# Bilinear feature interaction on one core: output buffers as pools of their own, eight instead of ten x blocks on GpSimd's queue, and one store split in two

## The chip, the core and the metric

The kernel runs on one core of a Trainium2 chip. The core has five instruction streams that run beside each other and meet only at semaphores: TensorE (PE, with its weight loads PEld), VectorE (DVE), ScalarE (ACT), GpSimd (POOL) and SyncE (SP). Three of them also start DMA transfers: SP, ACT and POOL each have a queue (in the profile q1 carries what SP starts, q10 what ACT starts, q0 what POOL starts), and all transfers run on the same 16 DMA engines. The metric is the time of one execution on the device in microseconds (us); lower is better.

## The reference

The input is x of shape [4096, 32, 64] (4096 rows of a batch, 32 fields, 64 numbers per field) and one 64x64 matrix W for each of the 496 pairs of fields i < j. For each row and each pair the kernel computes a vector of 64 numbers and writes them all:

```python
idx_i, idx_j = np.triu_indices(F, k=1)
vi = inputs[:, idx_i, :]
vj = inputs[:, idx_j, :]
vidots = jnp.einsum('bpd,pde->bpe', vi, W)
return vidots * vj
```

All numbers are float32. The inputs are 33.5 MB of x and 8.1 MB of W; the output is 4096 x 496 x 64 numbers, 520 MB. The output outweighs the input by more than ten to one.

## The kernel before, in words

The batch is cut into 16 blocks of 256 rows. A block holds two tiles, one row per partition each, so that there are 32 tiles of 128 rows. For one tile, all pairs (i, j) with the same i are neighbours in the output, so one product with field i against the matrices of several j gives up to 16 pairs at a time (a "step", L314: two matmuls, one for each half of the 64 result columns, into one PSUM buffer of two banks). The step's result is multiplied by the x fields j and lands in an output buffer in SBUF. For most steps DVE does this straight from PSUM (L330). For the first step of the fields i in `aside` (1, 3, 5, ..., 13), ACT copies PSUM to the output buffer (L327) and POOL multiplies there (L328), seven times for each tile.

Steps are gathered into groups of pairs; when a group is complete, SP stores it with one DMA (L335). The first three tiles (`LEAD = 3`) are cut into six groups each and run interleaved, group by group, while the weights still arrive. All later tiles are cut into four groups each of 118 to 127 pairs (3.8 to 4.2 MB per store) and run one after the other. Only the very first group of tile 0 is stored in two parts (`ends`).

The output buffers are all parts of one SBUF tile `ob` (L74), and `out_home` (L82) says by a running number n which part a group gets: three buffers in turn at first, four from n = 10 (`FOURTH`) to the end of the lead, and three larger ones from tile 3 on. The same tile also holds, in the beginning, the last raw rows of W and the reordered rows `rp` that TensorE transposes into the weight tile `wT`. The framework keeps track of which region of a tile an instruction reads and writes, and puts waits between them.

x lives in `xb`, five slots of one x tile each (L71). Blocks 0 and 1 are loaded by SP at the start. From then on, `loads` gives the moment: at the fifth step of the last tile of one pair of blocks (2e - 2 and 2e - 1), the next pair (2e, 2e + 1) is loaded. So there are seven such moments, e = 1 to 7. A block in the list `fifteen` (L110) is loaded by POOL with `load_fifteen`: one DMA of 120 partitions (L165), a tiny one over 17 partitions that turns POOL's queue on by one engine (`turn_engines`, L157), and two of the last 8 partitions. The code takes it that 120 partitions go to 15 of the 16 DMA engines, 8 rows of 16 KB each, so that one engine is spared, always the same. Any other block is loaded whole by ACT (L141), three steps later in the program. `slots_of` says which two slots a block takes. Before the change, the pairs at e = 1, 2, 4, 6 have one block on each queue (ACT the first, POOL the second), and the pairs at e = 3, 5, 7 have both blocks on POOL.

TensorE also transposes x: four fields' pairs at a time (L213), copied by ACT to a transposed buffer (L215 to L217) in two buffers of `xtb` (and, during the lead, in two more in slot 0 of `xb`).

The order of the instructions on each engine is the order of the program; the places of the loads, of the transposes (`AHEAD`) and of the weight work (`due`) are written out by hand. SP's queue holds nothing but loads at the start and then the stores in order; each store waits for the last DVE and POOL instruction of its part.

Of the kernel before, what the change touches and what calls it, by code (L numbers as in the profile page):

```python
# [8 lines left out]
F32 = mybir.dt.float32  # L9
# [3 lines left out]
def kernel(  # L13
# [17 lines left out]
    nc = tc.nc  # L31

    B, F, D = x.shape
    P = 128
# [5 lines left out]
    E2 = D // 2  # L40
    BANK = 512
    CH = BANK // E2
    RUN = 8
    p0 = [i * (F - 1) - i * (i - 1) // 2 for i in range(F)]
# [5 lines left out]
    wrows = list(zip(cuts[:-1], cuts[1:]))  # L50


    LEAD = 3
# [3 lines left out]
    for t in range(NT):  # L57
        b = lead if t < LEAD else later
        groups[t] = list(zip(b[:-1], b[1:]))
    cap0 = max(b - a for a, b in groups[0])  # L60
    cap1 = max(b - a for a, b in groups[LEAD])

    const = ctx.enter_context(tc.tile_pool(name="const", bufs=1))
# [5 lines left out]
    wT = const.tile([P, NP, E2], F32, tag="wT", name="wT")  # L69
    FD = F * D  # L70
    xb = const.tile([P, 5, FD], F32, tag="xb", name="xb")  # L71
    XT = 2 * (RUN // 2) * P
    xtb = const.tile([P, 2 * XT], F32, tag="xtb", name="xtb")
    ob = const.tile([P, 3 * cap1, D], F32, tag="ob", name="ob")  # L74

    FOURTH = 3 * len(groups[0]) - 8  # L80

    def out_home(n: int, later_: bool):  # L82
        if later_:
            o, c = (2 - n % 3) * cap1, cap1
        elif n < FOURTH:
            o, c = (0, 2, 1)[n % 3] * cap0, cap0
        else:
            k = 3 - (n - FOURTH) % 4
            o, c = k * cap0 if k < 3 else 3 * cap1 - cap0, cap0
        return ob[:, o : o + c, :]  # L90

    RAW, RP = P * E2 // D, 2 * BANK // D
    assert 3 * cap0 + RAW + 2 * RP <= 3 * cap1 and LEAD == 3 and FOURTH % 3 == 1

    xt_used = [0]

    def xt_home(t: int):
        n = xt_used[0]  # L100
        xt_used[0] += 1
        n = n % 4 if t < LEAD else n % 2
        mem, o = (xtb, n * XT) if n < 2 else (xb[:, 0], (n - 2) * XT)
        return mem[:, o : o + XT].rearrange("p (s u b) -> p s u b", s=2, b=P)

    fifteen = (3, 5, 6, 7, 9, 10, 11, 13, 14, 15)  # L110

    def slots_of(blk: int):
        e, second = divmod(blk, 2)
        if e == 0:
            return ((1, 2), (3, 4))[second]
        if e % 2 == 0:
            return ((2, 3), (1, 4))[second]
        if 2 * e in fifteen:
            return ((1, 3), (2, 0))[second]
        return ((1, 2), (3, 0))[second]  # L120

    def tile_of(t: int):

        blk, k = divmod(t, NB)
        a, b = slots_of(blk)
        return blk, k if a < b else 1 - k
# [5 lines left out]
    def x_tile(t: int):  # L132
        blk, k = tile_of(t)
        return x_block(blk)[:, k]
# [39 lines left out]
    wflat = w.rearrange("p d e -> p (d e)")  # L174
    EU = 2 * BANK // P
    NU = E2 // EU

    def raw_w(c: int):
        if c + 1 < len(wrows):
            a = wrows[c + 1][0]  # L180
            return wT[:, a : a + P, :].rearrange("p r e -> p (r e)")
        return ob[:, 3 * cap1 - RAW :, :].rearrange("p r e -> p (r e)")

    def load_w(c: int):
        a = wrows[c][0]
        nc.sync.dma_start(out=raw_w(c), in_=wflat[a : a + P])

    def order_w(c: int, k: int, copy):

        r = wrows[c][1] - wrows[c][0]  # L190
        o = cap0 + k * RP if c == 0 else 3 * cap1 - RAW - (1 + k % 2) * RP
        rp = ob[:, o : o + RP, :].rearrange("p r e -> p (r e)").rearrange("p (e h d) -> p e h d", h=2, d=D)
        src = raw_w(c)[:r].rearrange("p (d h e) -> p e h d", h=2, d=D)
        ins = copy(rp[:r], src[:, k * EU : (k + 1) * EU])  # L194
        if c > 0:
            tc.keep_in_program_order(ins)
        return rp
# [9 lines left out]
    def turn_x(t: int, q: int, copy):  # L207


        pt = psum.tile([P, RUN // 2, P], F32, tag="ps", name=f"ptx_{t}_{q}")  # L210
        for u in range(RUN // 2):
            f = q * RUN + 2 * u
            nc.tensor.transpose(pt[:, u, :], x_tile(t)[:, f : f + 2, :].rearrange("p f d -> p (f d)"), ident)  # L213
        xT = xt_home(t)
        copy(xT[:, 0], pt)  # L215
        copy(xT[D:, 1], pt[:D])  # L216
        copy(xT[:D, 1], pt[D:])  # L217
        return xT
# [58 lines left out]
    v, p, a = nc.vector.tensor_copy, nc.gpsimd.tensor_copy, nc.scalar.copy  # L277
    xT, rps = {}, {}
# [5 lines left out]
        if k == 3:  # L284
            xT[0, 0] = turn_x(0, 0, a)

    n_out = {}
    for s, (t, st) in enumerate(sched):
        blk, kt = tile_of(t)
        g, i, c0, m = steps[t][st]  # L290
        if s in loads:
            for b in (loads[s], loads[s] + 1):
                if b in fifteen:
                    load_fifteen(b)
        if s - 3 in loads and loads[s - 3] not in fifteen:
            tc.keep_in_program_order(load_x(loads[s - 3], nc.scalar))
        for what, *args in due.get(s, ()):
            if what == "x":
                xT[tuple(args)] = turn_x(*args, a)
            elif what == "turn":  # L300
                turn_w(*args, rps.pop(tuple(args)), a)
            else:
                c, k = args
                rps[c, k] = order_w(c, k, ((v, v, p, v), (v, v, p, a))[k % 2][c])

        base, end = groups[t][g]
        pa = p0[i] + c0
        if pa == base:
            ot = out_home(len(n_out), t >= LEAD)
            n_out[t, g] = ot  # L310
        ot = n_out[t, g]
        ps = psum.tile([P, 2, CH, E2], F32, tag="ps", name=f"ps_{s}")
        for h in range(2):
            nc.tensor.matmul(  # L314
                ps[:, h, :m, :],
                xT[t, i // RUN][h * D : (h + 1) * D, (i + h) % 2, i % RUN // 2, :],
                wT[h * D : (h + 1) * D, pa : pa + m, :],
                start=True,
                stop=True,
            )  # L320
        o = pa - base
        j = i + 1 + c0
        dst = ot[:, o : o + m, :].rearrange("p m (h e) -> p m h e", h=2)
        src = ps[:, :, :m, :].rearrange("p h m e -> p m h e")
        xj = x_tile(t)[:, j : j + m, :].rearrange("p m (h e) -> p m h e", h=2)
        if i in aside and c0 == 0:
            nc.scalar.copy(dst, src)  # L327
            nc.gpsimd.tensor_mul(dst, dst, xj)  # L328
        else:
            nc.vector.tensor_mul(dst, src, xj)  # L330

        ends = (p0[2], end) if (t, g) == (0, 0) else (end,)
        if pa + m in ends:
            n0 = p0[2] if len(ends) > 1 and pa + m == end else base
            nc.sync.dma_start(  # L335
                out=rows_of(out, blk).rearrange("(p k) n d -> p k n d", k=NB)[:, kt, n0 : pa + m, :],
                in_=ot[:, n0 - base : pa + m - base, :],
            )
# [28 lines left out]
```

## Time and profile before

| quantity | value |
|---|---|
| median of 5 runs | 1332.47 us (1330.3 to 1335.79) |
| profiled execution | 1330.3 us |
| its span, first to last instruction | 1328.5 us |
| bytes moved, mean rate | 563.17 MB, 424 GB/s |
| PE, DVE, ACT, POOL busy | 86%, 72%, 35%, 43% |
| mean granted TensorE clock | 0.948 |

The profile's page gives the busy share of each engine, then the span in 40 slices (the rows DMA and GB/s tell how busy the 16 DMA engines were in each slice and what they moved), the DMA queues, and the chain of work that ended last. Beside the page, the trace answers for any stretch of time: busy time of each engine, granted clock, mean busy share of the DMA engines and GB/s, and for each group of DMA issues the median time from issue to landing. A busy share of the DMA engines slightly over 1 in a stretch comes from packets that overlap a little. The trace also keeps each DMA packet with its start, length, size and queue. Each store ends with 16 packets of four bytes, one on each DMA engine, so their spread shows how far the 16 engines lie apart.

### The profile page before, as it was taken

Reading aid. Unit: us, or ns where it says so; the run is one execution under the profiler, and the core shown is the slowest. Engines: PE = TensorE matmul, PEld = TensorE weight load, DVE = VectorE, ACT = ScalarE, POOL = GpSimd, SP = SyncE. Lnnn points to the kernel's source line nnn. Section 1 sums busy time; section 2 is a strip of 40 time slices with the busy share of each in tenths; the row PEclk is TensorE's granted clock in tenths of the full one; section 3 lists DMA queues with packets and bytes.
Section 4 is the critical chain, followed back from the end, with each engine's and each line's share of the span. In section 5 each row is a group of like instructions: output and inputs, shape, how many; then the busy total and the mean of one; then the engine's idle time right before and its main releaser. Section 6 shows DMA issues by size and latency. Waiting matters only on the chain.

```text
span 1328.5 us, 17395 instructions
## 1 busy us (share of the span) xinstructions
PE 1141.2 (86%) x6644; PEld 600.3 (45%) x6644; DVE 951.3 (72%) x1287; ACT 471.3 (35%) x627; POOL 566.1 (43%) x276
## 2 busy tenths in 40 slices
PE   6999989997988978998788897798969988889884
PEld 4455445453444434444344444444434444444442
DVE  5679768774777766877577876678757777677773
ACT  4563324332333323333233332333323333233331
POOL 2861524445434444435344352444524445244440
PEclk9999989998999998999899999999989999889997
DMA  9999999999999999999999999999999999999998
GB/s 388 432 426 429 399 431 432 431 432 423 431 431 432 433 411 423 431 430 419 424 430 433 429 425 413 427 432 430 419 427 427 435 430 397 429 428 431 433 430 365
DMA packets 25170, 563.17 MB, mean 424 GB/s; under 512 B 3680, under 2 KB 3680, under 8 KB 4128
## 3 DMA queue, kind: packets, MB, share of 16 engines
q1 hardware_dynamic: 20448, 532.69, 93.9%
q0 software_dynamic: 4064, 21.00, 4.1%
q10 hardware_dynamic: 576, 8.39, 1.6%
q8 instruction: 52, 0.85, 0.2%
q14 instruction: 30, 0.25, 0.0%
HBM read 41.94 MB, written 520.09 MB: 423 GB/s over the span
## 4 chain that ended last, share of the span: by engine, by line
DMA 36%; PE 13%; DVE 5%; issue 3%; POOL 2%; ACT 2%; DVEq 0%; ACTq 0%; POOLq 0%
DMA out_dram<-ob 30%; PE ps L314 12%; DVE ob L330 5%; DMA xb<-in_r_inputs_dram 5%; POOL ob L328 2%; ACT ob L327 1%; PE ptx L213 1%; POOL xb L165 0%; POOL scratch L157 0%; ACT xtb L215 0%; ACT xtb L217 0%; ACT xtb L216 0%; DVEq L330 0%; ACTq L327 0%; DVEq L363 0%
## 5 line engine op out<-in xcount | busy, mean ns | idle before, releaser
L330 DVE TENSOR_TENSOR ob<-ps,xb 128x1024 f32<-128x1024 f32 (+4 forms) x1277 | 939.9, 791 | 345.5 <-DMA out_dram<-ob 176.0
L314 PE MATMUL ps<-wT,xtb 64*128 64x512 f32 (+15 forms) x5760 | 1013.1, 490 | 147.2 <-ACT ob L327 77.8
L328 POOL TENSOR_TENSOR ob<-ob,xb 128x1024 f32<-128x1024 f32 x224 | 528.5, 2364 | 734.4 <-ACT ob L327 717.9
L314 PEld LDWEIGHTS ps<-wT,xtb 64*128 64x128 f32 x5760 | 509.4, 195 | 613.5 <-DVE ob L330 230.3
L327 ACT COPY ob<-ps 128x1024 f32<-128x1024 f32 x224 | 226.8, 1012 | 479.7 <-PE ps L314 265.5
L215 ACT COPY xtb<-ptx 128x512 f32<-128x512 f32 x122 | 71.4, 585 | 315.5 <-PE ptx L213 315.5
L213 PE MATMUL ptx<-ident,xb 128*128 128x128 f32 x512 | 85.8, 291 | 8.6 <-DMA xb<-in_r_inputs_dram 6.6
L213 PEld LDWEIGHTS ptx<-ident,xb 128*128 128x128 f32 x512 | 55.2, 144 | 61.0 <-issue 31.7
L217 ACT COPY xtb<-ptx 64x512 f32<-64x512 f32 x122 | 71.0, 582 | 3.0
L216 ACT COPY xtb<-ptx 64x512 f32<-64x512 f32 x122 | 70.4, 577 | 3.0
L314 PE MATMUL ps<-wT,xb 64*128 64x512 f32 (+15 forms) x244 | 41.4, 460 | 1.0 <-ACT ob L327 0.3
L314 PEld LDWEIGHTS ps<-wT,xb 64*128 64x128 f32 x244 | 20.4, 186 | 17.4 <-issue 6.0
L204 PE MATMUL ptw<-ident,ob 128*128 128x128 f32 (+1 forms) x128 | 18.6, 298 | 10.9 <-DVE ob L194 10.4
L204 PEld LDWEIGHTS ptw<-ident,ob 128*128 128x128 f32 (+1 forms) x128 | 15.5, 157 | 16.7 <-issue 13.5
L165 POOL DMA_DIRECT2D xb<-in_r_inputs_dram x30 | 18.9, 631 | 0.0
L205 ACT COPY wT<-ptw 128x1024 f32<-128x1024 f32 (+1 forms) x15 | 14.9, 992 | 9.6 <-PE ptw L204 9.5
L194 DVE COPY ob<-wT 128x1024 f32<-128x1024 f32 (+1 forms) x7 | 7.1, 1040 | 8.9 <-DMA wT<-in_L_rec_W_dram 8.9
L157 POOL DMA_DIRECT2D scratch<-in_r_inputs_dram x12 | 11.1, 924 | 0.3 <-issue 0.3
L215 ACT COPY xb<-ptx 128x512 f32<-128x512 f32 x6 | 3.5, 588 | 13.4 <-PE ptx L213 13.3
L194 POOL COPY ob<-wT 128x1024 f32<-128x1024 f32 x4 | 7.8, 1963 | 0.0
L194 ACT COPY ob<-wT 112x1024 f32<-112x1024 f32 x1 | 2.0, 1966 | 6.9 <-DMA wT<-in_L_rec_W_dram 6.9
L194 DVE COPY ob<-ob 128x1024 f32<-128x1024 f32 x2 | 4.0, 2006 | 0.0
(11 smaller groups left out, 14.2 us busy)
## 6 DMA issues: line engine op xcount, KB each, us to landing
out_dram<-ob SPq DMA_DIRECT2D x29, 4064.0 KB, 18.8
out_dram<-ob SPq DMA_DIRECT2D x29, 4032.0 KB, 19.2
out_dram<-ob SPq DMA_DIRECT2D x29, 4000.0 KB, 20.4
out_dram<-ob SPq DMA_DIRECT2D x29, 3776.0 KB, 19.4
xb<-in_r_inputs_dram POOLq DMA_DIRECT2D x10, 1920.0 KB, 33.4
out_dram<-ob SPq DMA_DIRECT2D x3, 2912.0 KB, 14.8
xb<-in_r_inputs_dram ACTq DMA_DIRECT2D x4, 2048.0 KB, 22.8
out_dram<-ob SPq DMA_DIRECT2D x3, 2624.0 KB, 11.3
```

The costliest lines, as they stand in the source:

```text
L165: tc.keep_in_program_order(nc.gpsimd.dma_start(out=dst[ps, :, fs], in_=rows[ps, :, fs]))
L194: ins = copy(rp[:r], src[:, k * EU : (k + 1) * EU])
L204: nc.tensor.transpose(pt[:, n, :r], rp[:r, n].rearrange("p h d -> p (h d)"), ident[:r, :r])
L205: copy(wT[:, a:b, k * EU : (k + 1) * EU], pt[:, :, :r].rearrange("p e r -> p r e"))
L213: nc.tensor.transpose(pt[:, u, :], x_tile(t)[:, f : f + 2, :].rearrange("p f d -> p (f d)"), ident)
L215: copy(xT[:, 0], pt)
L216: copy(xT[D:, 1], pt[:D])
L217: copy(xT[:D, 1], pt[D:])
L314: nc.tensor.matmul(ps[:, h, :m, :], xT[t, i // RUN][h * D : (h + 1) * D, (i + h) % 2, i % RUN // 2, :], wT[h * D : (h + 1) * D, pa : pa + ...
L327: nc.scalar.copy(dst, src)
L328: nc.gpsimd.tensor_mul(dst, dst, xj)
L330: nc.vector.tensor_mul(dst, src, xj)
```

## The change

There are three edits.

1. `ob` is gone. Each output buffer is a tile pool of its own with one buffer: `o0` to `o2`, later `o3`, and `later0` to `later2` from tile 3 on. Raw weight rows and `rp` have pools as well, and pools are closed and opened where the buffers change. The transposed x has a pool of two. What a new tile in a pool has to wait for is then the release of the whole tile that was there before, once, and no longer region by region.
2. `fifteen` loses blocks 6, 10 and 14 and gains block 8. The pairs at e = 3, 5, 7 now have one block on ACT's queue and one on POOL's, and the pair at e = 4 has both on POOL's. `slots_of` follows.
3. The first group of tile 3 (the fourth tile) is stored in two parts, pairs of the fields 0 and 1 first.

```diff
-    xtb = const.tile([P, 2 * XT], F32, tag="xtb", name="xtb")
-    ob = const.tile([P, 3 * cap1, D], F32, tag="ob", name="ob")
+    xtpool = ctx.enter_context(tc.tile_pool(name="xtpool", bufs=2))
...
+    opools = out_pools(smaller, "o0", "o1", "o2")
+    (rawpool,) = out_pools(rows_in, "raw")
+    rpool = rows_in.enter_context(tc.tile_pool(name="rp", bufs=2))
+    n_out = [0]
+
+    def new_out(t: int, g: int):
+        n = n_out[0]
+        n_out[0] += 1
+        if n == FOURTH:
+            rows_in.close()
+            opools.extend(out_pools(smaller, "o3"))
+        if (t, g) == (LEAD, 0):
+            smaller.close()
+            opools[:] = out_pools(ctx, "later0", "later1", "later2")
+        if t >= LEAD:
+            k, cap = 2 - n % 3, cap1
+        else:
+            k, cap = (0, 2, 1)[n % 3] if n < FOURTH else 3 - (n - FOURTH) % 4, cap0
+        return opools[k].tile([P, cap, D], F32, tag="ot", name=f"ot_{t}_{g}")
...
-    fifteen = (3, 5, 6, 7, 9, 10, 11, 13, 14, 15)
+    fifteen = (3, 5, 7, 8, 9, 11, 13, 15)
...
-        if e % 2 == 0:
-            return ((2, 3), (1, 4))[second]
         if 2 * e in fifteen:
-            return ((1, 3), (2, 0))[second]
-        return ((1, 2), (3, 0))[second]
+            return ((1, 3), (2, 4 * (1 - e % 2)))[second]
+        return (((2, 3), (1, 4)), ((1, 2), (3, 0)))[e % 2][second]
...
-            ot = out_home(len(n_out), t >= LEAD)
-            n_out[t, g] = ot
-        ot = n_out[t, g]
+            ots[t] = new_out(t, g)
+        ot = ots[t]
...
-        ends = (p0[2], end) if (t, g) == (0, 0) else (end,)
+        ends = (p0[2], end) if (t, g) in ((0, 0), (LEAD, 0)) else (end,)
```

## The prediction

> **What bounds the kernel now.** I read the page's busy shares first, then the two rows on DMA, the queues, then stretches of the span with and without x loads, and last what POOL and SP do where the stretches are worst.
>
> ```profile
> PE 1141.2 (86%) x6644; PEld 600.3 (45%) x6644; DVE 951.3 (72%) x1287; ACT 471.3 (35%) x627; POOL 566.1 (43%) x276
> DMA  9999999999999999999999999999999999999998
> GB/s 388 432 426 429 399 431 432 431 432 423 431 431 432 433 411 423 431 430 419 424 430 433 429 425 413 427 432 430 419 427 427 435 430 397 429 428 431 433 430 365
> q1 hardware_dynamic: 20448, 532.69, 93.9%
> q0 software_dynamic: 4064, 21.00, 4.1%
> q10 hardware_dynamic: 576, 8.39, 1.6%
> ...
> out_dram<-ob SPq DMA_DIRECT2D x29, 4032.0 KB, 19.2
> xb<-in_r_inputs_dram POOLq DMA_DIRECT2D x10, 1920.0 KB, 33.4
> xb<-in_r_inputs_dram ACTq DMA_DIRECT2D x4, 2048.0 KB, 22.8
> ```
>
> The DMA row is 9 in every slice but the last, and the queues' shares add up to 99.6% of 16 engines. PE at 86% is the next, not the bound. So an engine's instruction costs time only where it leaves DMA engines without work; what counts is the rate at which they move bytes. A store of 4.13 MB takes 9.6 us at 431 GB/s and lands 19.2 us after its issue: about one other store is always queued ahead. The GB/s row dips at 399, 411, 419, 413, 419 and 397, where x is loaded. By stretches (the last two columns are the DMA share and GB/s):
>
> ```profile
> 360.00:440.00 80.00, 71.54 (x426) 36.92 (x424) 61.07 (x84) 29.70 (x40) 34.86 (x15) 0.98 1.01 432
> 1000.00:1100.00 100.00, 90.26 (x523) 46.57 (x520) 74.34 (x102) 37.16 (x50) 47.02 (x20) 0.95 1.00 430
> ...
> 135.00:185.00 50.00, 44.61 (x256) 23.40 (x256) 36.53 (x52) 16.83 (x23) 22.02 (x13) 0.93 1.01 410
> 295.00:345.00 50.00, 40.48 (x220) 20.72 (x220) 32.00 (x44) 15.08 (x20) 20.37 (x12) 0.90 1.00 424
> 455.00:535.00 80.00, 64.46 (x366) 33.45 (x366) 52.22 (x71) 24.97 (x33) 38.48 (x22) 0.94 1.00 420
> 615.00:665.00 50.00, 39.45 (x222) 20.40 (x222) 31.17 (x45) 15.63 (x22) 19.28 (x11) 0.90 1.00 417
> 785.00:865.00 80.00, 63.37 (x354) 33.04 (x352) 51.55 (x68) 25.37 (x34) 38.46 (x22) 0.94 1.00 419
> 945.00:995.00 50.00, 36.79 (x210) 18.55 (x208) 29.79 (x41) 14.06 (x19) 19.32 (x11) 0.90 1.01 420
> 1108.00:1188.00 80.00, 65.44 (x355) 34.34 (x354) 51.38 (x69) 24.64 (x32) 38.50 (x22) 0.89 1.00 416
> ```
>
> Without loads the rate is 430 to 432; I take 431. A stretch of length T at rate R loses T x (431 - R)/431. The pairs split over ACT and POOL at e = 2, 4, 6 (295, 615, 945) lose 0.8, 1.6 and 1.3 us, mean 1.24. The pairs with both blocks on POOL at e = 3, 5, 7 (455, 785, 1108) lose 2.0, 2.2 and 2.8 us, mean 2.35. The split pair at e = 1 (135), where tile 3 begins, loses 2.4. The DMA engines count as busy all the while: the loss is in how long their packets take.
>
> **The change part by part.**
>
> *Blocks 6, 10, 14 to ACT, block 8 to POOL.* Three pairs become split and one becomes POOL alone, net two pairs at 2.35 - 1.24 = 1.11 us: -2.2 us. Ends: the smallest against the largest loss of the two kinds gives 2.0 - 1.6 = 0.4 per pair (-0.8), the other way 2.8 - 0.8 = 2.0 (-4.0). The mean is taken, since seven stretches lie near it. Every issue counts: POOL loses 2 x 4 DMAs (0.78 + 0.98 + 0.56 + 0.57 = 2.9 us per block, its timeline below), ACT gains 2 issues of 0.33 us and their waits. Behind ACT's load stand its copies of transposed x and of PSUM. At e = 2, 4, 6 ACT's waits for this instruction last 17 to 38 ns each, and at e = 3, 5, 7 it will wait for the same kind of instruction (DVE's and POOL's last use of the slots), so 0; if the last POOL product (2.36 us) ended last each time, 3 x 2.4 us on an engine that is 35% busy, hidden by the queued store.
>
> The Trainium skill, "DMA: Bandwidth & Descriptors", section "Issuing engines are not separate DMA queues", speaks against this term: transfers started by different engines run on the same 16 DMA engines, and spreading them only saves the issuing sequencer's time. The landing rows (22.8 us on ACT's queue, 33.4 on POOL's) show more than issue time. By the rule this term would be 0, as POOL's 2.9 us per block are covered, and the sum 2.2 us higher.
>
> *First group of tile 3 in two stores.* The loss at e = 1 is almost all in eight microseconds:
>
> ```profile
> 144.00:148.00 4.00, 3.93 (x24) 1.99 (x22) 3.27 (x4) 2.76 (x4) 3.91 (x5) 1.00 0.98 349
> 148.00:152.00 4.00, 4.00 (x28) 2.42 (x26) 3.61 (x5) 1.01 (x1) 4.00 (x2) 1.00 1.00 312
> ...
> 140.24 2.36 POOL L328 TENSOR_TENSOR ob<-ob,xb 128x1024 f32<-128x1024 f32 x1 [29.57 <-ACT ob L327]
> 142.55 0.78 POOL L165 DMA_DIRECT2D xb<-in_r_inputs_dram  x1
> 143.33 0.99 POOL L157 DMA_DIRECT2D scratch<-in_r_inputs_dram  x1
> 144.31 1.13 POOL L165 DMA_DIRECT2D xb<-in_r_inputs_dram  x2
> 145.47 4.80 POOL L328 TENSOR_TENSOR ob<-ob,xb 128x1024 f32<-128x1024 f32 x2
> ```
>
> There the previous store has just run out (its packets end from 147.2 us), and the next is issued at 147.87, when POOL's second product of the group (i = 3) is done, 5.2 us late behind POOL's four load issues. The engines read x with no store beside: 4 x 82/431 + 4 x 119/431 = 1.9 us lost. The new first part (i = 0 and 1) needs only POOL's first product, done at 142.6. So a store of 2.0 MB (4.6 us) stands in the queue before the old one ran out. What stays is the ordinary price of a split pair: of the 2.44 us of this stretch 1.2 go, down to the mean of 1.24. Ends: -1.9 (the whole gap) and +0.3 (nothing gained, and SP's extra issue of 0.33 us on the path). SP has nothing else queued that is ready. I take -1.2.
>
> *The spared engine.* Two fewer `load_fifteen` put 2 x 8 rows of 16 KB more on the DMA engine that the code spares. By the queue's row an engine needs 0.041 x 16 x 1328.5/21.0 = 41.5 us per MB, 5.4 us for 0.131 MB, 10.9 in all; the other fifteen get 0.7 us less each. Whether that engine is the last one decides. The page has no row for it, but the trace's packets have. In stretches without loads one engine's 32,512-byte packets mostly take 1,227 to 1,265 ns, and the others' 1,204. Against the mean of all 16, it falls behind by 3.0% (from 0.0 us at 348 to 3.4 at 462; from -0.1 at 999 to 3.4 at 1112), and each load puts it forward again. From the last store before a split load to a clean one after, it went from 0.6 to 0.0 (281 to 348 us), 2.7 to 0.0 (625 to 664) and 2.5 to -0.1 (950 to 999): -2.0 on average, and with its 3.0% over 52 us, -3.6. POOL-only loads gave 3.4 to 0.0 (462 to 549), 3.4 to 0.0 (777 to 886) and 3.4 to -2.2 (1112 to 1219): -4.1, and with 101 us of drift -7.1. So each POOL load spares it about 3.5 us, and two fewer leave it 7.1 us later. Now it ends about 0.8 us after the mean, and the last engine 3.0 us after (the last store's 16 closing packets start from 1321.86 to 1326.90). Later it would end 7.9 after a mean that is itself as much earlier as the other terms say; the end comes 7.9 - 3.0 = 4.9 later, less the 0.7: +4.2. Ends: -0.7 (another engine stays last) and 10.9 + 0.8 - 3.0 = +8.7. I take +4.2, the measured recovery.
>
> "DMA: Bandwidth & Descriptors", section "Latency and other measured facts", says that two of the engines are usually slower, and guesses at GpSimd's descriptor rings. The 3.0% is there in stretches without any POOL load, which speaks against that as the whole cause; by the guess, fewer POOL loads would make the engine faster, and this term would be 0 or less.
>
> *Pools.* The order on PE and DVE is unchanged, and on ACT, POOL and SP only the loads and the added store move. DVE's separate wait instructions fall from 925 to 246 in the built program:
>
> ```profile
> L330 DVEq EVENT_SEMAPHORE  x921: 21/21/2327, 15.6 to 1305.9; - x185
> ```
>
> At 21 ns that is 14 us, 0.1 us per group, beside a queued store: 0. The end below nothing is the two store-starved places in the trace that the earlier issue could fill, at 0.14 us each (share 0.99), -0.3. Against it, a first write waits for the whole old buffer: group 0 of tile 0 had two stores (0.95 MB the second, 2.2 us), and n = 3 now waits for both. DVE is busy from 37.4 to 44.1 us without a gap there and then idles 4.1 us for a landing, so at most 0.5 us of delay vanishes in that idle time; if not, +2.2 us, as the stores of the lead have little queued ahead (share 0.99 from 80 to 100 us). From tile 3 on, one store frees one buffer either way.
>
> **Sum.** -2.2 - 1.2 + 4.2 + 0 = +0.8 us on the profiled execution's 1330.3, so 1331.1. The median of the runs shown is 2.2 us above that execution: 1333.3. I give 1333.0, without the last decimals.
>
> **Rivals.** (a) *The balance costs nothing* (chance 0.26): another engine remains last because the spared one is helped by less POOL traffic. For it: the trace's tail, where the last engine isn't the spared one; against it: the steady 3.0%. Then -2.2 - 1.2 - 0.7 = -4.1, and with the whole gap at tile 3, -4.8: 1327.7 to 1328.4, faster. (b) *The spared engine becomes the bound* (0.21), the other side: at its full 5.4 us a load the end moves +8.7, the sum is +5.3, 1337.8. It decides from 5.2 us per load on (2 x 5.2 + 0.8 - 3.0 - 0.7 - 3.4 = +4.1). Before the end it would show as landing times growing through the last third. For it: 8 rows at the queue's price; against: 3.5 measured over six loads. (c) *Whole-buffer waits* (0.05) add 2.2 us in the lead: 1335.2, within. (d) *The queue of a load doesn't matter* (in the forecast's range): the loss follows the bytes; then 0 for the first term, 1335.2.
>
> **The numbers.** About 0.3% (4 us) is what a measurement of this kernel can tell from no change: 1328.5 to 1336.5. Forecast with (d) 0.48, (c) 0.05: same 0.53. (a) faster 0.26, (b) slower 0.21. The range takes in (a)'s lower end and (b)'s value: 1327.5 to 1338. The forecast's own is 1330 to 1336.
>
> **What would show it.** Stretches of the new profile around the loads at e = 3, 5, 7 at about 420 GB/s over 50 us, and around e = 4 at 418 over 80; the 8 us after tile 3's first step at 400 or more; landing times of the stores rising by several us toward the end if the spared engine lags, and a last slice below 365 GB/s. Wrong would make it a DMA share under 0.97 in any slice, a landing on ACT's queue near 33 us at e = 3, 5, 7, or a spread of the last 16 packets that stays at 5 us.

## The result

The kernel before takes 1332.42 us (median), the changed one 1329.12 us. The ratio is 0.9978, with a 95% interval of 0.9973 to 0.9984: 2.9 us faster (2.1 to 3.6; the medians differ by 3.3). That is less than the 0.3% that the prediction took as its bound, but the interval leaves no doubt of the sign. The forecast was 1333.0 us, +0.8 us on the profiled execution. So the sign was wrong, by 3.7 us.

The profiled execution of the changed kernel took 1332.18 us (span 1330.4). It is the longest of its 33 runs, and 1.9 us longer than the profiled one of the kernel before, although the kernel is faster. So a comparison of these two executions alone says the opposite of the result. Why that is so is the first thing to read from the profile after.

The page of the changed kernel: the DMA row, the rate, the queues and the landing of the loads.

```profile
DMA  9999999999999999999999999999999999999997
GB/s 389 431 409 423 406 433 434 430 431 417 430 430 435 427 421 431 432 432 424 415 425 432 428 418 423 435 430 430 422 424 432 431 433 413 429 429 431 432 428 324
...
q1 hardware_dynamic: 20592, 532.69, 93.8%
q0 software_dynamic: 3264, 16.80, 3.2%
q10 hardware_dynamic: 864, 12.58, 2.3%
...
xb<-in_r_inputs_dram POOLq DMA_DIRECT2D x8, 1920.0 KB, 33.5
xb<-in_r_inputs_dram ACTq DMA_DIRECT2D x6, 2048.0 KB, 22.8
```

The DMA engines are still the bound. 4.2 MB have moved from POOL's queue (q0) to ACT's (q10). Two slices stand out against the page of before: the third (409, before 426) and the last (324, before 365). The loads come out close to the forecast. These are the stretches with x loads (the last two columns are DMA share and GB/s):

```profile
135.00:185.00 50.00, 41.14 (x250) 22.99 (x251) 34.95 (x51) 16.32 (x23) 19.29 (x11) 0.90 1.01 416
295.00:345.00 50.00, 37.83 (x220) 19.22 (x218) 31.35 (x42) 14.68 (x20) 19.31 (x11) 0.90 1.00 420
455.00:505.00 50.00, 38.98 (x218) 20.07 (x218) 30.21 (x45) 14.06 (x19) 19.28 (x11) 0.90 1.01 424
615.00:695.00 80.00, 64.84 (x376) 34.54 (x378) 53.28 (x74) 26.38 (x35) 37.20 (x22) 0.94 1.00 421
785.00:835.00 50.00, 39.37 (x224) 19.99 (x222) 32.33 (x44) 15.16 (x21) 21.67 (x12) 0.90 1.01 419
945.00:995.00 50.00, 40.10 (x220) 20.71 (x218) 31.81 (x43) 15.08 (x20) 19.71 (x12) 0.90 1.00 421
1108.00:1158.00 50.00, 40.61 (x222) 20.88 (x220) 32.31 (x43) 15.08 (x20) 19.53 (x12) 0.90 1.01 418
```

By the prediction's formula, T x (431 - R)/431, the six pairs from e = 2 on now lose 8.0 us, and lost 10.8 before: -2.8, where -2.2 was forecast. The pair at e = 1 loses 1.7 instead of 2.4: -0.7, where -1.2 was forecast. At that place, the two stretches of four microseconds now read

```profile
144.00:148.00 4.00, 4.00 (x26) 2.12 (x24) 3.39 (x4) 2.32 (x4) 3.98 (x6) 1.00 1.10 383
148.00:152.00 4.00, 3.93 (x26) 2.02 (x24) 3.43 (x5) 2.33 (x3) 3.99 (x3) 1.00 0.82 326
```

against 349 and 312 before. The store's first part is issued at 144.21 us, 4.3 us before the first engine runs dry; before, it came 1.0 us after. The rate stays below the 400 GB/s that was forecast.

Two things work against these gains in the profiled execution. First, the end. The 16 closing packets of the last store show when each DMA engine is done. On average they come at 1322.7 us (before 1323.9), but the last one at 1328.7 (before 1326.9): one engine ends 6.0 us after the mean instead of 3.0. This is the forecast's balance term, +3.1 of its +4.9. Second, a gap in the lead that nothing in the change explains. Here are the kernel before, then the changed one, in the stretches 66 to 72 us and 85 to 90 us (the third figure from the end is TensorE's granted clock):

```profile
66.00:72.00 6.00, 4.26 (x28) 2.53 (x28) 4.60 (x6) 4.32 (x4) 1.47 (x1) 1.00 1.01 430
85.00:90.00 5.00, 4.96 (x36) 2.67 (x36) 3.94 (x7) 2.02 (x2) 5.00 (x3) 1.00 1.01 431
```

```profile
66.00:72.00 6.00, 4.04 (x16) 2.14 (x17) 4.76 (x6) 3.63 (x4) 0.24 (x1) 0.72 1.01 432
85.00:90.00 5.00, 5.00 (x36) 2.76 (x34) 3.25 (x5) 2.63 (x3) 3.90 (x3) 1.00 0.73 310
```

The clock falls to 0.72 on average. TensorE sets the pace of the lead there, so the store at 89.1 us comes 1.8 us later than in the kernel before. All 16 engines have run dry by then (share 0.73), some 1.3 us in all. With the loads (-2.8), the store (-0.7), the end (+3.1) and this gap (+1.3) the sum is +0.9, of the +1.9 between the two profiled executions. Whether the last two belong to the kernel or to the one execution is what the experiments had to tell.

### The profile page after: what moved, and what is told of

Same layout as the page of the kernel before. It is cut to its first block, busy times and chain, and to the rows that moved or that the text cites. A ratio compares the mean times of both kernels' runs of the same rounds, so it can differ in the third digit from the quotient of the medians.

```text
span 1330.4 us, 16623 instructions
## 1 busy us (share of the span) xinstructions
PE 1138.1 (86%) x6644; PEld 597.2 (45%) x6644; DVE 950.4 (71%) x1287; ACT 471.3 (35%) x627; POOL 560.3 (42%) x268
## 5 line engine op out<-in xcount | busy, mean ns | idle before, releaser
L344 DVE TENSOR_TENSOR ot<-ps,xb 128x1024 f32<-128x1024 f32 (+4 forms) x1277 | 939.1, 791 | 347.5 <-DMA out_dram<-ot 184.3
L328 PE MATMUL ps<-wT,xT 64*128 64x512 f32 (+15 forms) x5760 | 1008.9, 488 | 154.4 <-ACT ot L341 78.2
L342 POOL TENSOR_TENSOR ot<-ot,xb 128x1024 f32<-128x1024 f32 x224 | 528.3, 2364 | 739.8 <-ACT ot L341 729.5
L328 PEld LDWEIGHTS ps<-wT,xT 64*128 64x128 f32 x5760 | 506.0, 194 | 619.8 <-DVE ot L344 247.4
L341 ACT COPY ot<-ps 128x1024 f32<-128x1024 f32 x224 | 226.9, 1013 | 479.9 <-PE ps L328 325.1
L230 ACT COPY xT<-ptx 128x512 f32<-128x512 f32 x122 | 71.4, 585 | 317.5 <-PE ptx L228 317.5
L232 ACT COPY xT<-ptx 64x512 f32<-64x512 f32 x122 | 71.0, 582 | 1.4
L231 ACT COPY xT<-ptx 64x512 f32<-64x512 f32 x122 | 70.4, 577 | 1.4
L219 PE MATMUL ptw<-ident,rp 128*128 128x128 f32 (+1 forms) x128 | 18.2, 293 | 10.9 <-DVE rp L209 10.2
L219 PEld LDWEIGHTS ptw<-ident,rp 128*128 128x128 f32 (+1 forms) x128 | 15.1, 153 | 17.0 <-issue 13.6
L209 POOL COPY rp<-wT 128x1024 f32<-128x1024 f32 x4 | 7.8, 1962 | 0.0
## 6 DMA issues: line engine op xcount, KB each, us to landing
out_dram<-ot SPq DMA_DIRECT2D x29, 4064.0 KB, 19.2
out_dram<-ot SPq DMA_DIRECT2D x29, 4000.0 KB, 20.2
xb<-in_r_inputs_dram POOLq DMA_DIRECT2D x8, 1920.0 KB, 33.5
xb<-in_r_inputs_dram ACTq DMA_DIRECT2D x6, 2048.0 KB, 22.8
```

The source lines that it names most:

```text
L219: nc.tensor.transpose(pt[:, n, :r], rp[:r, n].rearrange("p h d -> p (h d)"), ident[:r, :r])
L328: nc.tensor.matmul(ps[:, h, :m, :], xT[t, i // RUN][h * D : (h + 1) * D, (i + h) % 2, i % RUN // 2, :], wT[h * D : (h + 1) * D, pa : pa + ...
```

## The experiments

Theory A: the loads gain as forecast, and the balance of the DMA engines costs nothing. Theory B: the prediction's terms hold, and the gain is from the other edits. Theory C: the pools make the gain. Theory D: the spared engine is a slow one, and is the last at the end of the changed kernel. All differences below are (ratio - 1) x the time before on the same chip, with their intervals. The mean and the last of the 16 closing packets are those of each kernel's profiled execution.

| kernel | lists | two stores | pools | us to before | last engine after mean, us |
|---|---|---|---|---|---|
| before | ten | no | no | 0 | 3.0 |
| lists | eight | no | no | -0.3 (-1.5 to 0.8) | 4.5 |
| split | ten | yes | no | -0.4 (-1.9 to 1.2) | 3.6 |
| pools | ten | no | yes | -1.6 (-3.2 to -0.1) | 4.7 |
| no_pools | eight | yes | no | -2.5 (-4.0 to -1.2) | 6.0 |
| no_lists | ten | yes | yes | -1.6 (-3.1 to 0.0) | 3.9 |
| no_split | eight | no | yes | -2.3 (-3.5 to -1.1) | 5.5 |
| changed | eight | yes | yes | -2.9 (-3.6 to -2.1) | 6.0 |

### Each edit alone, and each left out

*The lists alone*, in the kernel before:

```diff
-    fifteen = (3, 5, 6, 7, 9, 10, 11, 13, 14, 15)
+    fifteen = (3, 5, 7, 8, 9, 11, 13, 15)
...
-        if e % 2 == 0:
-            return ((2, 3), (1, 4))[second]
         if 2 * e in fifteen:
-            return ((1, 3), (2, 0))[second]
-        return ((1, 2), (3, 0))[second]
+            return ((1, 3), (2, 4 * (1 - e % 2)))[second]
+        return (((2, 3), (1, 4)), ((1, 2), (3, 0)))[e % 2][second]
```

> The kernel before with the eight blocks on GpSimd and their slots alone (one of three edits); differences are to the kernel before. Theory A (the loads gain as forecast and the spared engine's balance costs nothing): -2.2 - 0.7 = -2.9 us. Theory B (the terms of the prediction hold, the balance costs +4.2, and the measured gain of 3.3 us is from the two other edits): +2.0 us. If the queue of a load and the balance are both worth nothing: 0.

*The two stores alone*, in the kernel before:

```diff
-        ends = (p0[2], end) if (t, g) == (0, 0) else (end,)
+        ends = (p0[2], end) if (t, g) in ((0, 0), (LEAD, 0)) else (end,)
```

> The kernel before with the first group of tile 3 in two stores alone. Prediction's term: -1.2 us. Theory A: between 0 and -1.2. Theory B needs more, the whole gap of 1.9 us or above it. In the profile the stretch from 144 to 152 us at 380 GB/s or more, and the slack of that store above 0 (it was issued 1.0 us after the first engines had run dry).

*The pools alone*: the changed kernel with both diffs above turned round.

> The pools alone: the changed kernel with the ten blocks, their slots and the single store of before. Prediction's term: 0 (bounds -0.3 and +2.2). Theory A: 0. Theory C (the pools make the gain, through 679 fewer waits on VectorE): -2 to -3.3 us. In the profile TensorE at full clock from 68 to 72 us if the low clock there in the changed kernel's profile was chance; low again if the pools cause it.

*Without the pools*: the kernel before with both diffs above.

> The two other edits without the pools (the one tile for all output buffers stays). Theories A and B: -3.3 us, as the whole change, or a little less. Theory C: no better than 0 to -1. If the profile of the changed kernel was delayed by 1.4 us by chance in the lead, this one shows no gap at 85 to 90 us; the spread of the last store's closing packets about 8 us if the spared engine's lag is what fewer GpSimd loads leave, about 5 us if not.

*Without the lists*: the changed kernel with the first diff turned round.

> The pools and the two stores, with the ten blocks of before on GpSimd. If the three edits add up by the runs of each alone (-0.3, -0.4, -1.6): -2.0 us. If the lists are what makes the gain once the store of tile 3 is no longer late (lists and split together gave -2.5, apart -0.3 and -0.4): -1.2 us or less of a gain. Theory B (the lists lose by the balance what they gain): -3.3 or better.

*Without the two stores*: the changed kernel with the second diff turned round.

> The pools and the eight blocks, with one store for the first group of tile 3. If the three edits add up by the runs of each alone: -1.9 us. Prediction's term for the store: -3.3 + 1.2 = -2.1 us. If lists and two stores only gain together: -1.6 us or less of a gain. In the profile the eight microseconds in which tile 3 begins at 330 to 350 GB/s again.

The table holds what was measured. Each edit is seen in four pairs of kernels that differ in it alone. The lists give -0.3, -2.1, -0.7 and -1.3 us, mean -1.1. The two stores give -0.4, -2.2, 0.0 and -0.6, mean -0.8. The pools give -1.6, -1.2, -2.0 and -0.4, mean -1.3. With intervals of about 1.2 us to either side for a kernel, such a mean of four differences is known to about 1.2 x 1.4 / 2 = 0.9 us. So no edit makes the gain alone; theories B and C both fall as wholes: the lists do not lose 2 us, and the pools are not the whole. Theory A's -2.9 for the lists is not there either. The two stores alone can't be told from nothing.

In the profile of the two stores alone the first part is issued in time at 144 us (its slack, the time from a store's issue to the moment the first engine runs dry, is 4.2 us), with 379 and 342 GB/s in the two short stretches, against 380 expected. In that of the pools alone there are 333 and 318. But the lists alone, with one late store, show 394 and 324 there, because their lead ends 1.7 us later; so these eight microseconds are no measure of the gain. Over the 50 us from 135 us six profiles with the two stores (two kernels with step 42, further down, among them) move 412 GB/s on average and six without 410, which is 0.2 us by the formula.

The column on the right tells what the balance costs. With ten blocks on POOL (six profiles, the two with step 42 further down among them) the last engine ends 2.5 to 4.7 us after the mean, 3.5 on average. With eight (six profiles) it ends 2.9 to 6.0 after it, 5.0 on average. So two fewer spared loads push the end out by 1.5 us against the mean, though the two ranges overlap. The mean itself comes 2.5 us earlier (1324.7 to 1322.2), and this contains the gain of the stores in four of the six against two of the six.

### The balance from the other side

*No sparing for two of the eight loads* of POOL:

```diff
-                if b in fifteen:
+                if b in (11, 13):
+                    tc.keep_in_program_order(load_x(b, nc.gpsimd))
+                elif b in fifteen:
                     load_fifteen(b)
```

> The changed kernel, but blocks 11 and 13 are loaded by GpSimd whole, over all 16 DMA engines, and spare none: 0.26 MB more on the engine that the list spares, 10.9 us by the price used in the prediction, 7.0 us by its measured recovery, and 0.7 us less on each of the others. Differences are to the kernel before (changed kernel: -3.3). Theory A (the spared engine doesn't set the end): -4.0 to -3.0 us. Theory B (it does, in the profile it ended 6.0 us after the mean): +3 to +7 us, landing times that grow to 26 us and more in the last third, and a spread of the last closing packets of 13 us or more.

Measured: 0.0 us to the kernel before (-1.1 to 1.2), so 2.9 worse than the changed kernel. The last engine ends 6.9 us after the mean. The balance is not free: theory A falls. But theory B's +3 to +7 are not reached, and the closing packets spread by 8.1 us, not 13. The stores land no later than in the changed kernel.

The run also settles a rival on the loads: that the late landing on POOL's queue comes from the four parts of a spared load and not from the queue. Its two whole loads on that queue (2048 KB each) land after 33.6 us, as late as the spared ones. The two stretches with these loads move 425 and 423 GB/s, against 419 and 421 in the changed kernel; from one profile it can't be told whether the four parts cost some of the rate.

*Seven blocks on POOL*, all pairs split:

```diff
-    fifteen = (3, 5, 7, 8, 9, 11, 13, 15)
+    fifteen = (3, 5, 7, 9, 11, 13, 15)
```

> The changed kernel with seven blocks on GpSimd (3, 5, 7, 9, 11, 13, 15): every pair split over the two queues, one spared load fewer. Differences are to the kernel before (changed kernel: -3.3). Theory A (a split pair costs 1.1 us less and balance is free): -4.4 to -4.8 us. Theory B (the spared engine sets the end, 3.5 us per load): -3.3 - 1.5 + 3.5 = -1.3 us. If the queue of a load is worth nothing and the balance too: -3.3.

Measured: -1.3 us (-2.7 to -0.1), as theory B has it, which counts a price for the balance: 1.6 worse than the changed kernel, with one load more on ACT's queue, where loads land sooner. The last engine ends 6.8 after the mean. The price per load is known only roughly: 2.9 for two loads is 1.4 each, and 1.6 plus the 1.1 that the load should have gained by its queue is 2.7. By the intervals these are uncertain by 0.7 and 1.5 us, so they need not disagree.

*The next engine spared instead*:

```diff
-    turn_engines(5)
+    turn_engines(6)
...
-    turn_engines(11)
+    turn_engines(10)
```

> The changed kernel with GpSimd's queue turned by six engines instead of five at the start (ten instead of eleven at the end): the eight loads spare the next DMA engine. Theory D (one engine is slower by 3% all along, and the eight loads of 3.5 to 5.4 us each are what keeps it level): +25 to +40 us to the kernel before, landing times that grow to 26 us and more soon after the first loads. If whichever engine is spared isn't the last one, and the lag of 3% belongs to the packets of any engine by chance: -3.3, as the changed kernel.

Measured: +25.4 us (23.6 to 27.3), 28.3 worse than the changed kernel. So one fixed engine is the slow one, and the eight loads keep it level: 28.3/8 = 3.5 us per load on average, the same as the recovery that the prediction had read from the trace. That the landing times grow, as expected, is not what happened. These are four of this kernel's stretches without loads:

```profile
360.00:440.00 80.00, 73.05 (x426) 37.82 (x426) 60.92 (x83) 28.94 (x39) 33.24 (x15) 0.96 0.99 423
700.00:780.00 80.00, 73.16 (x418) 38.20 (x420) 60.52 (x84) 29.07 (x40) 34.34 (x15) 0.94 1.00 430
1000.00:1100.00 100.00, 90.89 (x540) 46.40 (x536) 76.62 (x106) 35.67 (x50) 39.96 (x17) 0.98 0.99 420
1200.00:1300.00 100.00, 90.58 (x544) 46.52 (x542) 76.92 (x109) 37.18 (x51) 40.03 (x18) 0.98 0.98 419
```

The reader should see 419 to 423 GB/s in three of them, where the kernel before has 430 to 432, at a DMA share of 0.98 to 0.99: the other engines wait a little there. The last engine's lag behind the mean goes to 7.1 us by 350 us and then stays between 7 and 9 away from the loads. The one exception explains the second row: behind the pair that is loaded near 615 us the lag falls to about 2 us, from 700 to 780 us it grows back from 4 to 6, and while it is that small the rate is 430. In this profile the first engines run dry just as the next store is issued: the median slack is 0.85 us, against 5.0 in the changed kernel. The reading of this is that a store frees its buffer only when its last engine has landed it, and there are three buffers, so that the lag stops growing where the others are made to wait for it. The saturation is measured; that the three buffers cause it is argued, as no run has another number of them. Landing times are no sign of the slow engine here (19.6 to 20.7 us for the large stores, against 19.2 to 20.2), and the lag at the end is not proportional to what was taken from the engine.

*A store that spares the engine*. If the slow engine is the last by 5 us, one store of 3.9 MB that leaves it out would end the matter. The group (29, 0) was given to POOL's queue in the way of the spared loads:

```diff
+            if (t, g) in ((29, 0),):
+                half = (pa + m - n0) // 2
+                tc.keep_in_program_order(nc.gpsimd.dma_start(out=to[:SWR], in_=fr[:SWR]))
+                turn_engines(1)
+                tc.keep_in_program_order(nc.gpsimd.dma_start(out=to[SWR:, :half], in_=fr[SWR:, :half]))
+                tc.keep_in_program_order(nc.gpsimd.dma_start(out=to[SWR:, half:], in_=fr[SWR:, half:]))
+            else:
+                nc.sync.dma_start(out=to, in_=fr)
```

> The changed kernel, but one store (the first group of tile 29, issued near 1201 us) goes through GpSimd's queue as the spared loads do: 120 partitions, the tiny DMA, and the last 8 in two halves. It takes some 9 us of packets off the spared engine and puts 0.6 us on each of the others. Differences are to the kernel before (changed kernel: -3.3; mean over eight-block kernels in the profiles: last engine 5.5 us after the mean, the next 1.0 to 2.7). Theory D (in the changed kernel the spared engine is the last by 3 us and more, in most executions): -5.5 to -6.5 us, and a spread of the last closing packets of 4 us or less. Theory A (balance costs nothing there): -2.3 to -3.3 us. If a store on GpSimd's queue is issued late or slowly: above -2.3, with a dry place at 1200 to 1220 us.

Measured: +11.9 us (10.0 to 13.7), a miss by 17 us and more. The store on POOL's queue brought the pipeline to a stop. Stretches behind its issue at 1202.4 us:

```profile
1200.00:1210.00 10.00, 8.42 (x52) 4.36 (x50) 7.05 (x9) 3.77 (x5) 8.80 (x7) 1.00 1.00 396
1210.00:1220.00 10.00, 2.10 (x12) 1.03 (x12) 2.28 (x4) 1.01 (x1) 1.56 (x2) 0.78 1.01 290
1220.00:1230.00 10.00, 9.62 (x56) 4.83 (x52) 4.41 (x8) 4.05 (x6) 6.21 (x3) 0.88 0.94 285
1230.00:1240.00 10.00, 0.00 (x0) 0.00 (x0) 0.00 (x0) 1.46 (x3) 0.00 (x0) 0.63 1.03 377
1240.00:1260.00 20.00, 15.43 (x86) 9.06 (x88) 14.66 (x21) 2.78 (x5) 2.06 (x1) 0.76 0.52 220
```

The landing of the stores from 1195 to 1260 us (KB, and us from issue to landing), and the waits from 1205 to 1260 us (total, times, longest):

```profile
out_dram<-ot SPq DMA_DIRECT2D x1, 4000.0 KB, 31.3
out_dram<-ot POOLq DMA_DIRECT2D x1, 3540.0 KB, 32.8
out_dram<-ot POOLq DMA_DIRECT2D x2, 118.0 KB, 37.7
```

```profile
DVE ot L344 <- DMA out_dram<-ot: 23.4, 2, 15.7
```

From 1210 to 1230 us the DMA engines are busy (share 1.01 and 0.94) and move only 285 to 290 GB/s; the store lands after 33 to 38 us, as the loads on this queue do, and a store of SP beside it after 31. DVE waits 15.7 us for that buffer, TensorE does nothing from 1230 to 1240, and the DMA engines run dry: from 1240 to 1260 us their share is 0.52. About half of what this place loses is lost there. So nothing can be told from this run's time on theory D. Nor do its closing packets tell anything, although the last engine ends only 1.4 us after the mean, with all 16 within 2.0 us: once the engines had run dry, the closing packets of the next store, at 1265 us, stand within 0.2 us of each other, and so any lag from before was gone, spared or not.

### The lead

*Step 42's matmuls three times over* (they write the same values again), so that TensorE has no idle time from 66 to 68 us:

```diff
-        for h in range(2):
+        for h in (0, 1) * (3 if s == 42 else 1):
             nc.tensor.matmul(
```

> The changed kernel with the two matmuls of step 42 issued three times over (same result), so that TensorE has no idle time of 2 us at 66 us in the lead. In 7 of 10 profiles the granted clock fell to 0.5 to 0.6 there for 3.4 us, and the store at 89 us was 1.2 to 1.3 us late with all engines dry. If this idle time is the cause: full clock from 66 to 74 us, no gap at 85 to 90 us, and -4.0 to -4.6 us to the kernel before (changed kernel: -3.3, times 0.7 of 1.3 us). If the clock falls without idle time too, or the extra matmuls delay the step as much: -3.3 or less of a gain.

Measured: -3.5 us (-4.8 to -2.1) in the changed kernel, 0.6 better than without, which the intervals can't tell from nothing. The four kernels that were run with and without this edit (three more follow) are 0.4 us better with it on average. What the low clock is tied to shows in the profiles. TensorE's timeline of the kernel before, of the lists alone, and of the changed kernel (start, us, and in brackets the idle time ahead):

```profile
67.74 2.09 PE L314 MATMUL ps<-wT,xtb 64*128 64x288 f32 x12 [2.13 <-DVE ob L330]
```

```profile
67.78 3.73 PE L312 MATMUL ps<-wT,xtb 64*128 64x288 f32 x12 [1.82 <-DVE ob L328]
```

```profile
67.96 3.46 PE L328 MATMUL ps<-wT,xT 64*128 64x288 f32 x12 [2.01 <-DVE ot L344]
```

The same twelve matmuls, after the same wait for DVE of about 2 us, take 2.1 us at the full clock, and 3.3 to 3.7 where it falls to half. The lists alone have nothing changed that runs before 70 us, and yet the clock falls. So the gap in the changed kernel's profile belongs to the execution, not to the change. Without the threefold step, 7 of 12 profiles have it (the expectations on record say 7 of 10; of those ten it was six); with it none of six. The changed kernel with the step:

```profile
66.00:72.00 6.00, 5.88 (x34) 2.90 (x34) 4.71 (x6) 4.71 (x5) 1.31 (x1) 1.00 1.03 440
85.00:90.00 5.00, 5.00 (x38) 2.74 (x37) 4.04 (x7) 2.02 (x2) 4.97 (x3) 1.00 1.00 428
```

The Trainium skill, "TensorE: Matmul & The Clock Gate", section "Part 1: The HAM clock gate (the "warmup" mystery)", says that the clock follows TensorE's activity in a free-running window of 3.4 us, and that idle time of a window closes it. The traces agree on the window: all changes of the granted clock in a trace lie on a grid of 3.41 us, and the grid starts at another phase in each execution. This phase tells the profiles apart. In the changed kernel a window runs from 65.05 to 68.46 us, the whole pause of 2.01 us lies in it, and the clock is at half from 68.46 us on, for one window. In the kernel before a boundary at 66.46 us cuts the pause of 2.13 us into 0.86 and 1.27, and nothing falls. So it is in all twelve: in the seven with a fall the pause (1.7 to 2.2 us) lies wholly in one window, in the five without a boundary cuts it (once with 1.73 of 1.83 us on one side). On the idle time the page differs: it names an idle window, and here about half a window was followed by a fall.

The same edit in the kernel before, with the pools alone, and with the lists and stores alone takes the lead out of the comparison:

> The kernel before with step 42's matmuls three times over, so that its lead has TensorE's full clock in every execution. If the low clock in most executions of the kernel before (its own profile had none) costs up to 1.3 us: -0.7 to -1.3 us to the kernel before. If not: 0.

> The pools alone, with step 42 three times over. Pools alone gave -1.6 us. Theory C1 (the pools gain by fewer waits on VectorE all along): 1.0 to 1.6 us better than the kernel before with the same edit. Theory C2 (they only made a low clock in the lead rarer): no better than that kernel.

> The lists and the two stores without the pools, with step 42 three times over. The changed kernel with the same edit gave -3.5 us by its ratio. Theory C1: 1 us worse than that, -2.5. Theory C2: the same, -3.5. Together with the kernel before under the same edit it gives the lists' and the store's share with the lead out of play: -2.0 us by the means of the runs so far (-1.5 and -0.5).

Measured: -0.8 us (-2.0 to 0.4), -1.6 (-2.9 to -0.3) and -2.8 (-4.0 to -1.5). With the changed kernel's -3.5, the pools give -0.8 and -0.7, and the lists and stores together -2.0 and -1.9, where the prediction had +0.8 for them. For the pools this lies between C1 and C2, and the two pairs, each uncertain by 1.8 us, decide for neither; over all six pairs the mean is -1.1. Of the twelve profiles without the threefold step, three of the four without the pools have the low clock and four of the eight with them. At 1.3 us for each, that would be worth 0.3 us.

*Both, and with seven blocks.* Two more kernels combine step 42 with the spared store, the second with seven blocks and a spared store for tile 15 as well (places `((15, 0), (29, 0))`).

> Both of the edits above in the changed kernel. If both theories hold: -6.5 to -7.5 us to the kernel before; if only the balance: -5.5 to -6.5; if only the clock: -4.0 to -4.6; if neither: -3.3.

> Every pair split (seven blocks on GpSimd), step 42 three times over, and two stores spared, the first groups of tiles 15 and 29. With seven blocks alone the difference to the kernel before was -1.3, 2.0 worse than the changed kernel, with its last engine 6.8 us after the mean. Theory D: the balance is repaid by the stores and the split pair's 1.1 us are left: 0.5 to 1 us better than the changed kernel with both edits, -7 to -8. If a pair's queue was not what the eight blocks gained by: no better than that kernel. Theory A: -1 to -2.5.

Measured: +11.3 us (9.6 to 12.9) and +43.0 (41.2 to 44.9). Both are ruled by the spared store's price, so they tell nothing of the queue of a load. All 16 engines end within 2.0 us in both.

## Why the prediction was wrong

| term, us | forecast | measured |
|---|---|---|
| loads on ACT's queue and balance | -2.2 + 4.2 | -1.1 (-1.9 by rates, +0.8 by closing packets) |
| first group of tile 3 in two stores | -1.2 | -0.8 (-0.2 by rates) |
| pools | 0 | -1.3 (-1.1 over six pairs) |
| sum | +0.8 | -3.2; the whole change -2.9 |

*Loads on ACT's queue: held.* -2.2 was forecast from the rates, and -2.8 came out of the same rates in the two profiles. Over the six profiles of each list, the pairs from e = 2 on lose 10.2 us with ten blocks and 8.3 with eight, which is -1.9. The landing of 22.8 us at every ACT load is as before, and the rates at e = 4 and at e = 3, 5, 7 are what was forecast (421 for 418, and 424, 419, 418 for 420). The rule of the Trainium skill, "DMA: Bandwidth & Descriptors", section "Issuing engines are not separate DMA queues", would have made this term 0; the -1.9 us and the landing rows (22.8 us on ACT's queue, 33.5 on POOL's) speak against that. In the time alone the queue can't be seen apart from the balance, since each load moved changes both.

*Two stores: the issue held, the size is not shown.* The store is now 4.3 us ahead of the engines instead of 1.0 behind. But the rate beside the loads did not come to 400 GB/s, the 50 us around them gain 0.2 us by their rates, and the mean of four pairs, -0.8 for -1.2, is within its error of both this and the forecast.

*The balance: this is the step that failed*, in the sentence "Later it would end 7.9 after a mean that is itself as much earlier as the other terms say; the end comes 7.9 - 3.0 = 4.9 later". Its premises held: one fixed engine is slower, and a load gives it 3.5 us, since sparing the wrong one costs 28.3 us for eight loads. What did not hold is that the whole 7.1 us of two loads stand at the end, on top of the 0.8 us of one execution. Six profiles with eight blocks have the last engine 2.9 to 6.0 us after the mean, six with ten blocks 2.5 to 4.7: +1.5 between the averages, not +4.9. The slow engine itself, told by its long packets, ends about 3 to 6 us after the mean with eight blocks and not 7.9; in the changed kernel's profile it is the last one, and in that of the same kernel with step 42 another engine is. With +1.5 - 0.7 for +4.2 the sum would have been -2.6 without the pools; and with the -1.9 of the rates this +0.8 gives the -1.1 that the time shows for the lists.

Why the lag stays below the sum is open. It shrinks where the other engines run dry and the slow one works on, but the changed kernel's profile has no such place above 0.6 us after 90 us, and it ends at 6.0. The saturation was met only at 7 to 9 us, with the wrong engine spared.

*Pools: the second miss.* The forecast had DVE's fewer waits hidden beside a queued store, and so at 0. The separate wait instructions of DVE's multiplications fell as forecast:

```profile
L344 DVEq EVENT_SEMAPHORE  x242: 21/50/2336, 15.0 to 1300.2; - x121
```

against 921 before. But the runs gain 0.4 to 2.0 us in all six pairs. Where in the span this gain lies was not shown: the profiles of a pair differ more by their dry places than by this. That the pools only made the low clock in the lead rarer is not excluded by the two pairs with the threefold step (-0.8 and -0.7, each uncertain by 1.8 us).

*The base.* The sum was made against an execution at 1330.3 us without the low clock in the lead; most profiles have it. The 2.2 us that were added for the median may have carried a part of this without a name (with the threefold step the kernel before is 0.8 us faster, uncertain by 1.2), and adding them was right.

*The rivals.* (a), at -4.1, is nearest to the result in time, but its reason is wrong: the balance does cost something, as the 2.9 and 1.6 us of the two experiments with less sparing show. That it comes so near has to do with the pools, which it put at nothing. (b), the spared engine as the bound, did not happen; it is what the kernel shows that spares the wrong engine. (c) did not happen: the store of n = 3 is issued at 47.4 us in the lead, and at 47.3 before. (d) is against the rates; the time alone does not decide on it. The range of 1327.5 to 1338 us holds the result.

What stays open: the price of one spared load near the changed kernel's place (1.4 to 2.7 us, with wide intervals), why the lag at the end is smaller than the sum, and the place of the pools' gain.

## What to carry to other kernels

Where all DMA engines are busy and one is slower, measure what a shift of work to it costs before adding it whole to the end. Here two loads less of sparing moved the last engine by 1.5 us and not 4.9, while with none left the full 3.5 us per load were paid, as a lower rate in the stretches, and neither the landing times nor the lag at the end showed its size. A term of the sum that is read at the end of one execution (which engine was last, and by how much) needs a second profile; here it was 2.5 to 4.7 us for the same list. And look at the granted clock in each stretch of both profiles before comparing them: a fall that is not in the change can be larger than the effect looked for.

## What was not expected of the hardware

- A pause of TensorE of 1.7 to 2.2 us was followed by half the clock (twelve matmuls in 3.3 to 3.7 us instead of 2.1) in 7 of 12 profiles, and in the other five, at the same place, it was not. In the seven it lay wholly in one of the 3.41 us windows of the clock's changes, in the five it was cut by a boundary.
- A store of 3.9 MB on GpSimd's queue took the rate of the 16 engines from about 431 to 285 to 290 GB/s for 20 us, at a busy share of 0.94 to 1.01, and landed after 33 to 38 us. Two loads of half that size on the same queue, in the kernel before, leave 377 to 400 GB/s in the lowest 20 us beside them (e = 3, 5 and 7).
- One DMA engine of the 16 is slower all along, and only one: with the next engine spared instead, in eight loads of 2 MB, the time is 28.3 us longer, and the last store's closing packets stand within 1.5 us but for one, which comes 7.4 us after their mean.
- A pair with both blocks on POOL is followed in some executions, some 80 us later, by a place where the engines run dry. In the profile of the kernel without the lists, behind the pair at e = 5, ACT waits 5.6 us for a store to land, TensorE pauses, its clock falls to 0.50, and the store at 866 us finds its first engines dry for 4.0 us:

```profile
ACT ot L343 <- DMA out_dram<-ot: 5.6, 1, 5.6
```

```profile
850.00:855.00 5.00, 1.46 (x12) 0.69 (x8) 1.50 (x4) 0.94 (x1) 0.94 (x1) 0.88 1.00 425
855.00:860.00 5.00, 4.87 (x18) 2.65 (x19) 2.16 (x4) 1.09 (x2) 4.00 (x2) 0.50 1.03 444
860.00:865.00 5.00, 5.00 (x32) 2.58 (x32) 3.22 (x7) 2.76 (x4) 1.96 (x2) 0.93 0.95 409
```

Three of the six profiles with ten blocks have first engines dry by 2.4 to 4.0 us at 862 to 866 us, and four by 0.4 to 1.6 us at 1186 to 1192 us, behind the pair at e = 7; none of the six with eight has either. That the pair causes it is read from this coincidence. So a part of what the lists gain may lie outside the stretches from which the term was made.
